# Two graph layers on 32 pairs of graphs: work of the first two and last two rounds reordered on ScalarE, VectorE and GpSimd, degrees of pair 1 found earlier, features asked for at a round's beginning

## The chip, the core and the metric

The kernel runs on one core of one Trainium2 chip. The metric is device time in microseconds of the whole program. Other cores are not used. Engines are named as in the profile: PE is TensorE's matmul (PEld its weight load), DVE is VectorE, ACT is ScalarE, POOL is GpSimd, SP is SyncE, which here only issues DMAs.

## The reference

There are 64 graphs of 256 nodes with 512 features, `x` (64, 256, 512) and `adj` (64, 256, 256), all float32. Two layers, each with a residual:

```
h = relu(layernorm(x));  q, k, v = h Wq^T + bq, h Wk^T + bk, h Wv^T + bv
w = adj * exp(q k^T);    x = x + (w / rowsum(w)) v
h = relu(layernorm(x));  A = adj + I;  d = rowsum(A)^-0.5
x = x + (d A d^T) (h W + b)
```

The output is the last `x`.

## The kernel before

Two graphs make a pair; 32 pairs (`NP`) are worked one after another. All products are float32 on PE. Each product of 2 by 2 blocks is done with seven block products in place of eight (sums before, sums after), so every stage has seven numbered steps; `left_sums` and `right_sums` form the operands, S1 to S4 and t1 to t4.

Stages of a pair, each a function that returns its seven steps:
- `query_stage` (g): gT, the features times a merged query and key weight. Its operands are hT, the turned features, and hS, their sums (`find_feature_sums`). Its results are summed for the next stage by `find_query_sums` (gS).
- `value_stage` (v): v, the values. `find_value_sums` makes two more operands from them, in vS.
- `score_stage` (s): scores, exponentials on ACT (`exponentials`) and the product with `adj` with its row sums on DVE (`mask`). Then `scale_weights` divides by the row sums, `turn_weights` transposes 32 by 32 blocks on DVE (eq), `move_weights` puts these blocks in place with sixteen copies (wT), and `find_weight_sums` makes wS on POOL.
- `output_stage` (o): weights times values, added into x.
- `neighbour_stages` (l and w): the second layer. l is the adjacency (aT, aS) times the second norm's features (h_b, hbS), w that times the weight W, added into x with the factor d.

Around them: `measure` (bn_stats and bn_aggr on DVE, then `inverse_root` and offsets on POOL) and `norm_features` (ACT) make the first layer's h_a in place of the loaded features; `turn_blocks` (DVE, hq) and `move` (sixteen ACT copies) turn it into hT. `measure_again` and `second_norm` do the same for the second layer (st_b, nb_b, h_b), and `find_node_sums` makes hbS. `degrees` sums the rows of `adj` on DVE, finds d on POOL, and by way of a small DRAM tile (dflat, written by SP) spreads d over all partitions (drow, read back by SP); `weigh_degrees` multiplies it with `adj` (ad) and gives ds, the factor of the bias in `add_graph_bias`. `turn_adjacency` transposes `adj` (aq to aT) and asks for the next pair's aq. `find_adjacency_sums` adds the diagonal and makes aS on POOL. `add_value_bias` is a DMA of POOL's queue that adds bv into x.

The order of the work is written by hand. `run` walks a string such as "g1 g5 g6 ..."; each token issues one block product (all of line 514, chained in this order on PE), the copies that read it, and then the calls listed under that token, placed on their engines behind the last instruction that reads a product. Each engine works its queue in order. Round p (`work_around(p)`) runs g, v and s of pair p + 1 with o, l and w of pair p. Ahead of round 0 is a run-in: weights are merged, pair 0 is prepared, and its g, v and s run alone. The last round, p = 30, also holds the O, L and W steps of pair 31, after which nothing is left to overlap. Where the string leaves instructions of one engine free against each other, the scheduler of the language orders them, and it gives buffers: h_a and h_b share three buffers (tag "h"), drow has one, `adj` (a) two, aq one.

Copies matter for the waits: steps 1, 6, 7 and 4 of a stage add into one PSUM bank, and ACT or DVE must have read the bank before the next of them begins.

Of the kernel before, what the change touches and what calls it, by code (L numbers as in the profile page):

```python
# [9 lines left out]
F32 = mybir.dt.float32  # L10
# [6 lines left out]
def kernel(  # L17
# [35 lines left out]
    nc = tc.nc  # L53
    P = 128
    B, N, D = x.shape
    G = 2
    NP = B // G
# [3 lines left out]
    TB = G * NB  # L61
    NT = G * N
# [8 lines left out]
    hp = ctx.enter_context(tc.tile_pool(name="hp", bufs=3))  # L71
# [36 lines left out]
    def load_blocks(p):  # L108

        q_tiles[p] = p1.tile([P, NB, G * N // Q, Q], F32, tag="aq", name=f"aq_{p}")
        blocks = adj[G * p : G * p + G].rearrange(
            "g (j c) (kt i r) -> i c kt (g j) r", c=Q, i=NQ, r=Q
        )
        for i in range(NQ):
            nc.sync.dma_start(q_tiles[p][i * Q : (i + 1) * Q], blocks[i])
# [26 lines left out]

    def load_the_rest():
        load_features(2)
        load_blocks(0)
        load_x(0)
        load_x(1)  # L150
        w1_view = w1.rearrange("(j t p) (i f) -> i j p t f", p=P, t=2, f=HD)
        nc.sync.dma_start(w1_set[:, A11], w1_view[0, 0])
        nc.sync.dma_start(w1_set[:, A12], w1_view[0, 1])
        nc.sync.dma_start(w1_21, w1_view[1, 0])
        nc.sync.dma_start(w1_set[:, A22], w1_view[1, 1])
        nc.sync.dma_start(b1_all, b1.partition_broadcast(P))
# [82 lines left out]
    def transpose_value_weight():  # L239
# [11 lines left out]


    norms, deg, ds, terms, blocks, hTs, parts, second, sides = ({} for _ in range(9))
    gTs, query_parts, weights, row_sums, turned, wTs, weight_parts, value_parts, aTs = (
        {} for _ in range(9)
    )

    def inverse_root(src, plus, name, tag="ir_r"):

# [6 lines left out]
    def scale_offset(xt, name, order, scale=None):  # L266

        mv = sm.tile([P, TB, 2], F32, tag="mv", name=f"mv_{name}")
        for t in order:
            st = sm.tile([P, 6], F32, tag="st", name=f"st_{name}_{t}")  # L270
            nc.vector.bn_stats(st, xt[:, t, :])  # L271
            nc.vector.bn_aggr(mv[:, t, :], st)
        rd = inverse_root(mv[:, :, 1], EPS, name)
        if scale is not None:
            rs = sm.tile([P, TB], F32, tag="rs", name=f"rs_{name}")
            nc.gpsimd.tensor_tensor(rs, rd, scale, mult)
            rd = rs
        nm = sm.tile([P, TB], F32, tag="nm", name=f"nm_{name}")
        nc.gpsimd.tensor_scalar(nm, mv[:, :, 0], -1.0, None, mult)
        nb = sm.tile([P, TB], F32, tag="nb", name=f"nb_{name}")  # L280
        nc.gpsimd.tensor_tensor(nb, nm, rd, mult)  # L281
        return rd, nb
# [12 lines left out]
    def measure(p):  # L295
        norms[p] = scale_offset(feats[p], f"a{p}", range(TB))
# [4 lines left out]
    def measure_again(p):  # L301
        norms[p] = scale_offset(x_tiles[p], f"b{p}", (2, 3, 0, 1), deg[p][0])

    def second_norm(p):
        second[p] = hp.tile([P, TB, D], F32, tag="h", name=f"h_b{p}")
        normed(second[p], x_tiles[p], *norms[p])


    def degrees(p):

        sums = sm.tile([P, TB], F32, tag="deg", name=f"deg_{p}")
        nc.vector.tensor_reduce(sums, a_tiles[p], AX.X, add)
        d = inverse_root(sums, 1.0, f"d{p}", "d")
        flat = dr.tile([NT], F32, tag="drow", name=f"dflat_{p}")
        nc.sync.dma_start(flat.rearrange("(t p) -> p t", p=P), d)
        row = p1.tile([P, NT], F32, tag="drow", name=f"drow_{p}")
        nc.sync.dma_start(row, flat.partition_broadcast(P))
        deg[p] = d, row

    def weigh_degrees(p):  # L320

# [135 lines left out]
    def find_value_sums(p):  # L457

        b11, b21, b22, t1, t2, t3, t4 = value_parts[p]
        eng = nc.gpsimd if p < NP - 1 else nc.vector  # L460
        eng.tensor_tensor(t2, b22, t1, sub)
        last = eng.tensor_tensor(t4, b21, t2, sub)
        if eng is nc.gpsimd:
            read(last)

    def turn_adjacency(p):

# [48 lines left out]
    def read(ins):  # L516
        last_read[ins.ins.engine] = ins.ins
        return ins
# [446 lines left out]
    def work_around(p):  # L965
        work = {
            "g1": [(move_weights, p, 8, 16)],
            "g6": [(find_weight_sums, p), (move, p + 2, 0, 4)],
            "g7": [(move, p + 2, 4, 6)],
            "o5": [(weigh_degrees, p + 1)],  # L970
            "o6": [(move, p + 2, 6, 10), (find_terms, p + 2)],
            "o7": [(move, p + 2, 10, 12), (degrees, p + 2), (add_value_bias, p + 1)],
            "v1": [(move, p + 2, 12, 16)],
            "o3": [(find_adjacency_sums, p), (measure_again, p)],
            "v5": [(find_query_sums, p + 1)],
            "v7": [(second_norm, p), (find_node_sums, p), (load_features, p + 3)],
            "v3": [(find_value_sums, p + 1)],
            "s3": [(load_a, p + 3)],
            "l7": [(measure, p + 3)],
            "l4": [(scale_weights, p + 1)],  # L980
            "l3": [(find_feature_sums, p + 2)],
            "w2": [(turn_weights, p + 1)],
            "w6": [(norm_features, p + 3)],
            "w5": [(turn_adjacency, p + 1)],
            "w7": [(move_weights, p + 1, 0, 8)],
            "w3": [(turn_blocks, p + 3)],
            "w4": [(add_graph_bias, p), (store, p), (load_x, p + 2)],
        }
        if p == 0:

            work["g6"] = [(find_weight_sums, 0)]
            work["g2"] = [(weigh_degrees, 0), (degrees, 1)]
            work["g7"] = []
            work["o5"] = []
            work["o6"] = [(norm_features, 2), (find_terms, 1), (turn_blocks, 2)]
            work["o7"] = [
                (move, 2, 0, 2),
                (add_value_bias, 1),
                (lambda p: weight_sums(w1_set, w1_21, nc.gpsimd), 0),
            ]  # L1000
            work["v1"] = [(move, 2, 2, 10), (weigh_degrees, 1), (degrees, 2)]
            work["v6"] = [(move, 2, 10, 16)]
        if p == 1:
            work["g2"] = [(find_terms, 2)]
        return work
# [2 lines left out]
    bs, g_rows, last = bias_products()  # L1008
    with tc.issue_after(last):
        measure(0)  # L1010
        measure(1)
        degrees(0)
        load_the_rest()
        c_rows, last = weighted_rows(wq_rows, bkT, "U2")
    with tc.issue_after(last):
# [14 lines left out]
        {  # L1030
            "g1": [(lambda p: weight_sums(v_set, v21), 0)],
            "g6": [(norm_features, 1)],
            "g7": [(turn_blocks, 1), (find_terms, 0)],
            "g4": [(move, 1, 0, 6)],
            "g3": [(find_query_sums, 0)],
            "v6": [(move, 1, 6, 7)],
            "s1": [(move, 1, 7, 12)],
            "s3": [
                (move, 1, 12, 16),
                (scale_weights, 0),  # L1040
                (find_feature_sums, 1),
                (turn_weights, 0),
                (load_a, 2),
            ],
            "v7": [(add_value_bias, 0)],
            "v2": [(move_weights, 0, 0, 8)],
            "v4": [(lambda p: nc.scalar.copy(b1_row, b1_all), 0)],
            "v3": [(turn_adjacency, 0), (measure, 2), (find_value_sums, 0)],
        },
    )  # L1050
    for p in range(NP - 2):
# [7 lines left out]
    p = NP - 2  # L1059
    ends = later(neighbour_stages, NP - 1)  # L1060
    run(
# [3 lines left out]
        {**around(p), "O": later(output_stage, NP - 1), "L": ends, "W": ends},  # L1065
        {
# [1 line left out]
            "g6": [(find_weight_sums, p)],  # L1068
            "o5": [(weigh_degrees, p + 1)],
            "o7": [(add_value_bias, p + 1)],  # L1070
            "o3": [(find_adjacency_sums, p), (find_query_sums, p + 1), (measure_again, p)],
            "s3": [(scale_weights, p + 1, nc.vector), (turn_weights, p + 1)],
            "v7": [(second_norm, p), (move_weights, p + 1, 0, 8, nc.gpsimd)],
            "v4": [(find_node_sums, p)],
            "v3": [(move_weights, p + 1, 8, 9), (find_value_sums, p + 1)],
            "l1": [(move_weights, p + 1, 9, 16), (find_weight_sums, p + 1)],
            "l3": [(turn_adjacency, p + 1), (find_adjacency_sums, p + 1)],
            "O3": [(measure_again, p + 1)],
            "w2": [(second_norm, p + 1), (find_node_sums, p + 1)],
            "w7": [(add_graph_bias, p)],  # L1080
            "w4": [(store, p)],
            "L6": [(add_graph_bias, p + 1)],
# [42 lines left out]
```

## Time and profile before

| | |
|---|---|
| median of 3 runs | 1817.01 us (1814.77 to 1819.02) |
| profiled execution | 1822.04 us, its span 1820.3 us |
| PE busy | 1789.2 us (98%), 9978 matmuls |
| DVE, ACT, POOL busy | 1331.5, 1165.2, 1191.4 us |
| mean granted PE clock | 0.996 |
| chain that ended last | PE 91% |

The span runs from the first to the last instruction; 1.7 us of the execution lie outside it. The numbers of a wait row are the total, the count and the longest, in us. A row of the timeline gives start, duration, engine, line, operation, output and inputs, count, and, in brackets, how long the engine was idle before and who ended that. A row of the stretches gives the stretch, its length, busy time and number of instructions of the engine, the granted PE clock, the share of the DMA engines and GB/s. Line numbers are those of the kernel before.

### The profile page before, as it was taken

What the parts mean: (1) busy time and instruction counts of PE and PEld (TensorE: products, weight loads), DVE (VectorE), ACT (ScalarE), POOL (GpSimd) and SP (SyncE); (2) the same over time, 40 slices, a digit from 0 to 9 for tenths busy, and PEclk for the clock granted to TensorE, in tenths of its full rate; (3) what the DMA queues carried; (4) which work ended last, traced back from release to release, by engine and by line L of the source; (5) the groups of instructions that cost most, each with busy time, mean ns of one, the idle gap of its engine ahead of it and who ended that gap; (6) DMA issues with size and microseconds to landing.
All of it is one profiled execution on the core that took longest, in us unless ns stands there. A gap on an engine that the chain in (4) does not pass through costs nothing.

```text
span 1820.3 us, 29061 instructions
## 1 busy us (share of the span) xinstructions
PE 1789.2 (98%) x9978; PEld 1618.9 (89%) x9978; DVE 1331.5 (73%) x3053; ACT 1165.2 (64%) x2326; POOL 1191.4 (65%) x1313
## 2 busy tenths in 40 slices
PE   9989999999999999999999999999999999999997
PEld 8888989999989989989999889999889999899986
DVE  6777777777777678777778787777787777777666
ACT  4765677666677656777666667666766666676532
POOL 2567576676666676766776766776766776766654
PEclk9999999999999999999999999999999999999999
DMA  6623543544543454434445434445435345335321
GB/s 180 150 76 87 113 91 100 114 84 110 111 90 103 103 95 111 100 92 112 97 99 113 94 93 116 86 104 118 85 98 120 76 110 121 83 99 122 64 48 47
DMA packets 245843, 182.58 MB, mean 100 GB/s; under 512 B 155456, under 2 KB 175936, under 8 KB 245696
## 3 DMA queue, kind: packets, MB, share of 16 engines
q1 hardware_dynamic: 227680, 146.11, 28.4%
q0 software_dynamic: 16960, 33.56, 15.0%
q8 instruction: 80, 1.31, 0.3%
q10 hardware_dynamic: 1056, 1.05, 0.2%
q14 instruction: 67, 0.55, 0.1%
HBM read 147.07 MB, written 33.62 MB: 99 GB/s over the span
## 4 chain that ended last, share of the span: by engine, by line
PE 91%; DVE 3%; DMA 2%; ACT 1%; POOL 1%; issue 1%; SPq 0%; DVEq 0%; ACTq 0%; POOLq 0%
PE pm_w L514 21%; PE pm_g L514 20%; PE pm_v L514 20%; PE pm_s L514 10%; PE pm_l L514 10%; PE pm_o L514 10%; DMA h_a<-in_x_dram 1%; DMA dflat<-irr_d 0%; DVE st_a L271 0%; DMA b_qk<-in_L_gnn_Wk_b_dram 0%; DMA drow<-dflat 0%; ACT wT L450 0%; DVE ad L327 0%; ACT h_b L287 0%; DVE st_b L271 0%
## 5 line engine op out<-in xcount | busy, mean ns | idle before, releaser
L514 PE MATMUL pm_w<-w_set,yS 128*128 128x256 f32 x1792 | 401.4, 381 | 8.3 <-DVE yS L879 3.8
L514 PEld LDWEIGHTS pm_w<-w_set,yS 128*128 128x128 f32 x1792 | 336.5, 191 | 53.2 <-DVE yS L879 4.8
L382 ACT COPY hT<-hq 32x512 f32<-32x512 f32 x496 | 305.6, 616 | 8.9 <-DVE hq L363 1.2
L514 PE MATMUL pm_v<-v_set,hT 128*128 128x256 f32 x1024 | 238.2, 381 | 0.8 <-ACT U_v L640 0.8
L514 PE MATMUL pm_g<-hT,m_set 128*128 128x256 f32 x1024 | 236.7, 379 | 0.0
L838 DVE SCALAR_TENSOR_TENSOR x<-pm_w,irr_d,x 128x256 f32<-128x256 f32 x256 | 110.9, 474 | 164.9 <-POOL x L848 113.9
L514 PEld LDWEIGHTS pm_g<-hT,m_set 128*128 128x128 f32 x1024 | 194.6, 190 | 26.9 <-ACT v L247 0.2
L514 PEld LDWEIGHTS pm_v<-v_set,hT 128*128 128x128 f32 x1024 | 193.1, 191 | 26.3 <-ACT U_v L640 1.2
L450 ACT COPY wT<-eq 32x256 f32<-32x256 f32 x504 | 202.3, 401 | 5.9
L514 PE MATMUL pm_v<-v_set,hS 128*128 128x256 f32 x768 | 177.9, 382 | 3.7 <-ACT A_v L649 3.7
L514 PE MATMUL pm_g<-hS,m_set 128*128 128x256 f32 x768 | 176.2, 379 | 0.0
L514 PEld LDWEIGHTS pm_v<-v_set,hS 128*128 128x128 f32 x768 | 144.4, 191 | 22.8 <-ACT A_v L649 4.5
L514 PEld LDWEIGHTS pm_g<-hS,m_set 128*128 128x128 f32 x768 | 146.0, 190 | 19.8
L763 POOL TENSOR_TENSOR x<-x,A_o 128x512 f32<-128x512 f32 x62 | 81.8, 1319 | 111.2 <-ACT A_o L761 110.2
L871 POOL TENSOR_TENSOR yS<-yS,U_l 128x512 f32<-128x512 f32 x32 | 40.7, 1272 | 120.9 <-DVE yS L870 117.1
L689 ACT ACTIVATE e<-e,ks 128x128 f32<-128x128 f32 x192 | 66.5, 395 | 83.0 <-DVE e L727 43.5
L287 ACT ACTIVATE h_b<-x,nb_b,rs_b 128x512 f32<-128x512 f32 x128 | 93.7, 802 | 24.7 <-POOL nb_b L281 24.7
L514 PE MATMUL pm_l<-aT,h_b 128*128 128x128 f32 x768 | 101.3, 275 | 1.7 <-POOL wS L388 1.7
L388 POOL TENSOR_TENSOR wS<-wT 128x256 f32<-128x256 f32 x32 | 23.4, 731 | 121.3 <-ACT wT L450 118.4
L514 PE MATMUL pm_s<-hT,gT 128*128 128x128 f32 x768 | 101.3, 275 | 1.4 <-DVE e L710 1.4
L514 PEld LDWEIGHTS pm_s<-hT,gT 128*128 128x128 f32 x768 | 97.9, 192 | 5.3 <-DVE e L710 2.2
L757 DVE TENSOR_TENSOR x<-pm_o,x 128x512 f32<-128x512 f32 x128 | 87.5, 686 | 18.3 <-PE pm_o L514 17.7
(180 smaller groups left out, 3938.5 us busy)
## 6 DMA issues: line engine op xcount, KB each, us to landing
h_a<-in_x_dram SPq DMA_DIRECT2D x64, 512.0 KB, 7.5
x<-in_x_dram SPq DMA_DIRECT2D x64, 512.0 KB, 4.4
x<-in_L_gnn_Wv_b_dram POOLq DMA_DIRECT2D x32, 1024.0 KB, 11.1
out_dram<-x SPq DMA_DIRECT2D x62, 512.0 KB, 3.5
a<-in_adj_dram SPq DMA_DIRECT2D x64, 256.0 KB, 3.1
aq<-in_adj_dram SPq DMA_DIRECT2D x128, 128.0 KB, 3.6
drow<-dflat SPq DMA_DIRECT2D x32, 256.0 KB, 6.3
wq_w<-in_L_gnn_Wq_w_dram ACTq DMA_DIRECT2D x2, 512.0 KB, 10.3
```

Source lines behind the costliest of these rows:

```text
L287: nc.scalar.activation(h[:, t, :], xt[:, t, :], AF.Relu, bias=nb[:, t : t + 1], scale=rd[:, t : t + 1],)
L382: nc.scalar.copy(dst[j * Q : (j + 1) * Q, i], src[i * Q : (i + 1) * Q, j])
L388: eng.tensor_tensor(s1, a21, a22, add)
L450: copy(dst[j * Q : (j + 1) * Q, i], src[i * Q : (i + 1) * Q, j])
L514: last_product[0] = nc.tensor.matmul(*args, **kwargs).ins
L689: nc.scalar.activation(block(qb, kb)[:, g], scores[:, g], AF.Exp, bias=terms[p][:, t : t + 1])
L757: read(nc.vector.tensor_tensor(block(n, i), bank, block(n, i), add))
L763: read(eng.tensor_tensor(block(n, i), block(n, i), more, add))
L838: nc.vector.scalar_tensor_tensor(to, bank[:, r, :], factor(n, r), to, mult, add)
L871: read(nc.gpsimd.tensor_tensor(t2, b22, t["part"], sub))
```

## The change

- Degrees: `degrees` is cut in two. `degrees(p)` finds d and writes dflat; `spread_degrees(p)` reads it back as drow. In the regular rounds the second half moves from o7 to s3. `degrees(0)` goes ahead of `measure(1)`, tied to the end of the first measuring; `spread_degrees(0)` goes behind feature load 2. `degrees(1)` goes from round 0 to g2 of the run-in, `spread_degrees(1)` and `weigh_degrees(0)` to its v3; `weigh_degrees(1)` and `degrees(2)` go from v1 to o7 of round 0.
- Features: `load_features(p + 3)` goes from v7 to g6. Ahead of it `claim(p)` now takes h_b's tile, which `second_norm` took itself before.
- Run-in: `scale_weights(0)` goes from ACT to DVE; the last four `move` copies of pair 1 and its `find_feature_sums` go from s3 to v7, so behind the copy A_v.
- Round 0: the `move` copies of pair 2 are spread 2, 5, 4, 5 over o7, v1, v6 and v7, where they were 2, 8 and 6 over o7, v1 and v6.
- Last round: v7 comes ahead of v2; the O steps begin between l7 and l3, with a new order among them. `find_value_sums(31)` goes from DVE to POOL. `measure_again(30)` goes from o3 to s6, `second_norm(31)` and `find_node_sums(31)` from w2 to w6, and `find_adjacency_sums(31)` from l3 to w6; the `move_weights` copies of ACT are split 4 and 4 over v3 and l1, where they were 1 and 7.

Of the instructions of PE only the last round's have another order. In the program as built, SP's queue in the run-in and round 0 reads: a(1), dflat(0), features 2, drow(0), aq(0), x(0), x(1), the second layer's weights, dflat(1), features 3, half of aq(1), a(2), the rest of aq(1), drow(1), dflat(2), drow(2), a(3), features 4. Before, it read: a(1), features 2, dflat(0), aq(0) with drow(0) after its first part, x(0), x(1), the weights, most of aq(1), a(2), the rest, dflat(1), drow(1), dflat(2), drow(2), features 3, a(3). In later rounds dflat, drow, features, a, aq keep their places, but the features are one pair further on.

```diff
     def load_the_rest():
         load_features(2)
+        spread_degrees(0)
         load_blocks(0)
...
+    def claim(p):
+
+        second[p] = hp.tile([P, TB, D], F32, tag="h", name=f"h_b{p}")
+
     def second_norm(p):
-        second[p] = hp.tile([P, TB, D], F32, tag="h", name=f"h_b{p}")
         normed(second[p], x_tiles[p], *norms[p])
...
         d = inverse_root(sums, 1.0, f"d{p}", "d")
-        flat = dr.tile([NT], F32, tag="drow", name=f"dflat_{p}")
-        nc.sync.dma_start(flat.rearrange("(t p) -> p t", p=P), d)
+        flats[p] = dr.tile([NT], F32, tag="drow", name=f"dflat_{p}")
+        nc.sync.dma_start(flats[p].rearrange("(t p) -> p t", p=P), d)
+        deg[p] = d, None
+
+    def spread_degrees(p):
+
         row = p1.tile([P, NT], F32, tag="drow", name=f"drow_{p}")
-        nc.sync.dma_start(row, flat.partition_broadcast(P))
-        deg[p] = d, row
+        nc.sync.dma_start(row, flats[p].partition_broadcast(P))
+        deg[p] = deg[p][0], row
...
         b11, b21, b22, t1, t2, t3, t4 = value_parts[p]
-        eng = nc.gpsimd if p < NP - 1 else nc.vector
-        eng.tensor_tensor(t2, b22, t1, sub)
-        last = eng.tensor_tensor(t4, b21, t2, sub)
-        if eng is nc.gpsimd:
-            read(last)
+        nc.gpsimd.tensor_tensor(t2, b22, t1, sub)
+        read(nc.gpsimd.tensor_tensor(t4, b21, t2, sub))
...
-            "g6": [(find_weight_sums, p), (move, p + 2, 0, 4)],
+            "g6": [(find_weight_sums, p), (move, p + 2, 0, 4), (claim, p), (load_features, p + 3)],
...
-            "v7": [(second_norm, p), (find_node_sums, p), (load_features, p + 3)],
+            "v7": [(second_norm, p), (find_node_sums, p)],
             "v3": [(find_value_sums, p + 1)],
-            "s3": [(load_a, p + 3)],
+            "s3": [(spread_degrees, p + 2), (load_a, p + 3)],
...
         if p == 0:
 
-            work["g6"] = [(find_weight_sums, 0)]
-            work["g2"] = [(weigh_degrees, 0), (degrees, 1)]
+            work["g6"] = [(find_weight_sums, 0), (claim, 0), (load_features, 3)]
...
             work["o7"] = [
                 (move, 2, 0, 2),
+                (weigh_degrees, 1),
+                (degrees, 2),
                 (add_value_bias, 1),
                 (lambda p: weight_sums(w1_set, w1_21, nc.gpsimd), 0),
             ]
-            work["v1"] = [(move, 2, 2, 10), (weigh_degrees, 1), (degrees, 2)]
-            work["v6"] = [(move, 2, 10, 16)]
+            work["v1"] = [(move, 2, 2, 7)]
+            work["v6"] = [(move, 2, 7, 11)]
+            work["v7"] = [(move, 2, 11, 16)] + work["v7"]
...
         measure(0)
+        with tc.issue_after(measured[-1]):
+            degrees(0)
         measure(1)
-        degrees(0)
         load_the_rest()
...
+            "g2": [(degrees, 1)],
...
-            "s3": [
-                (move, 1, 12, 16),
-                (scale_weights, 0),
-                (find_feature_sums, 1),
-                (turn_weights, 0),
-                (load_a, 2),
+            "s3": [(scale_weights, 0, nc.vector), (turn_weights, 0), (load_a, 2)],
+            "v7": [(move, 1, 12, 16), (find_feature_sums, 1), (add_value_bias, 0)],
+            "v2": [(move_weights, 0, 0, 8)],
+            "v3": [
+                (turn_adjacency, 0),
+                (weigh_degrees, 0),
+                (spread_degrees, 1),
+                (measure, 2),
+                (find_value_sums, 0),
+                (lambda p: nc.scalar.copy(b1_row, b1_all), 0),
             ],
-            "v7": [(add_value_bias, 0)],
-            "v2": [(move_weights, 0, 0, 8)],
-            "v4": [(lambda p: nc.scalar.copy(b1_row, b1_all), 0)],
-            "v3": [(turn_adjacency, 0), (measure, 2), (find_value_sums, 0)],
...
-        "g1 g5 g6 g2 g7 o1 o5 g4 o6 g3 o2 o7 v1 o4 o3 v5 v6 s1 s6 s5 s7 s2 s4 s3 v2 v7 v4 v3 "
-        "l1 l2 l6 l5 l7 l4 l3 O1 O5 O6 O7 O4 O2 O3 w1 w2 w6 w5 w7 w3 w4 "
+        "g1 g5 g6 g2 g7 o1 o5 g4 o6 g3 o2 o7 v1 o4 o3 v5 v6 s1 s6 s5 s7 s2 s4 s3 v7 v2 v4 v3 "
+        "l1 l2 l6 l5 l7 O1 l4 O5 l3 O6 O2 O7 O3 O4 w1 w2 w6 w5 w7 w3 w4 "
         "L1 L2 L6 L5 L7 W1 L4 L3 W2 W6 W5 W7 W3 W4",
...
-            "o3": [(find_adjacency_sums, p), (find_query_sums, p + 1), (measure_again, p)],
+            "o3": [(find_adjacency_sums, p), (find_query_sums, p + 1)],
+            "s6": [(measure_again, p)],
             "s3": [(scale_weights, p + 1, nc.vector), (turn_weights, p + 1)],
-            "v7": [(second_norm, p), (move_weights, p + 1, 0, 8, nc.gpsimd)],
+            "v7": [(claim, p), (second_norm, p), (move_weights, p + 1, 0, 8, nc.gpsimd)],
             "v4": [(find_node_sums, p)],
-            "v3": [(move_weights, p + 1, 8, 9), (find_value_sums, p + 1)],
-            "l1": [(move_weights, p + 1, 9, 16), (find_weight_sums, p + 1)],
-            "l3": [(turn_adjacency, p + 1), (find_adjacency_sums, p + 1)],
-            "O3": [(measure_again, p + 1)],
-            "w2": [(second_norm, p + 1), (find_node_sums, p + 1)],
+            "v3": [(move_weights, p + 1, 8, 12), (find_value_sums, p + 1)],
+            "l1": [(move_weights, p + 1, 12, 16), (find_weight_sums, p + 1)],
+            "l3": [(turn_adjacency, p + 1)],
+            "O4": [(measure_again, p + 1)],
+            "w6": [
+                (claim, p + 1),
+                (second_norm, p + 1),
+                (find_adjacency_sums, p + 1),
+                (find_node_sums, p + 1),
+            ],
```

More of the change, by code (lines that the diff above doesn't have):

```diff
@@ L253 @@
     norms, deg, ds, terms, blocks, hTs, parts, second, sides = ({} for _ in range(9))
-    gTs, query_parts, weights, row_sums, turned, wTs, weight_parts, value_parts, aTs = (
-        {} for _ in range(9)
+    flats, gTs, query_parts, weights, row_sums, turned, wTs, weight_parts, value_parts, aTs = (
+        {} for _ in range(10)
     )
+    measured = []
     def inverse_root(src, plus, name, tag="ir_r"):
@@ L271, in scale_offset @@
             nc.vector.bn_stats(st, xt[:, t, :])
-            nc.vector.bn_aggr(mv[:, t, :], st)
+            last = nc.vector.bn_aggr(mv[:, t, :], st)
+        measured.append(last.ins)
         rd = inverse_root(mv[:, :, 1], EPS, name)
```

## The prediction

> **What bounds the kernel now.** I read the busy shares first: PE is busy 1789.2 of 1820.3 us, so at most 31.1 us can be won, less what must stay. Then the chain of waits, filtered to PE (total, times, longest):
>
> ```profile
> PE pm_s L514 <- DVE s L336: 4.7, 1, 4.7
> PE pm_w L514 <- DVE yS L879: 3.8, 2, 2.9
> PE pm_v L514 <- ACT A_v L649: 3.7, 2, 2.9
> ...
> PE pm_w L514 <- ACT U_w L847: 3.0, 1, 3.0
> PE pm_l L514 <- POOL wS L388: 1.7, 1, 1.7
> ```
>
> All are single events. By the timeline PE idles 3.5 us at the start, 4.0 at the end, and else at 23.3 (0.8), 54.3 (2.9), 87.7 (0.8), 91.4 (4.7), 171.5 (2.9), 656.7 and 670.6 (0.3, 0.9) and from 1748.7 to 1793.8 in eight pieces (10.3). The rounds between repeat every 54.86 us (pm_g at 239.78 and 294.64) without a gap. So only the edges and two places in the middle can pay.
>
> A gap costs more than its length. By stretches, PE's busy time and granted clock:
>
> ```profile
> 54.30:57.24 2.94, 0.01 (x1) 1.00 1.13 240
> 57.24:62.65 5.41, 5.41 (x17) 0.68 0.58 107
> ...
> 171.46:174.34 2.88, 0.01 (x1) 1.00 0.10 33
> 174.34:176.00 1.66, 1.66 (x4) 0.56 0.00 0
> ```
>
> Sixteen pm_v took 5.41 us where sixteen take 3.45 elsewhere in the chain: 1.96 lost to the clock. Likewise 1.86 after 91.4, 1.96 after 171.5, 2.0 after the pair at 1765 to 1769; nothing after the 3.05 at 1787.4. The Trainium skill (TensorE: Matmul & The Clock Gate, What's actually happening) says the clock halves after an idle window of about 3.4 us, free-running. By it alone only the 4.7 gap would cost extra, about 1.7 us; the rows show four such losses, 7.8 us. I take the rows: a gap near 3 us costs 1.9 more, three times in four.
>
> **First pair (ScalarE).** v4 at 54.3 waits for A_v, queued on ACT behind four hT moves (2.50) and four row scalings (1.70). The scalings go to VectorE (1.14 in the last round's row), the moves behind A_v. The exponentials end at 52.47 and v7 at 52.4, so A_v ends at 53.1, before 54.3: 2.9 + 1.96 = 4.9 won. Cover: the moves now end at 55.6, g1 starts at 57.65; eq is done at 55.8, the sixteen wT moves at 63.35, before o1 at 66.3. Four scalings delay VectorE's v sums, which it catches up by 63.5; a late hT move would cost PE what it exceeds 2.1 us by.
>
> **Degrees of pair 1 (VectorE, GpSimd, SP).** The gS sums of round 0 stood behind weigh_degrees(1):
>
> ```profile
> 75.90 8.43 DMA dflat<-irr_d
> 84.35 7.20 DMA drow<-dflat
> ...
> 91.56 0.96 DVE ad L327 x2
> ```
>
> The reduction (1.2) moves to g2 of the run-in, where VectorE idles 1.40 at 35.2: free. On SP, dflat(0) now stands ahead of feature load 2, which goes from 13.8 to about 21.6, needed at 66.4: free. Then drow(0), aq, x, weights come about 7 us sooner; dflat(1) is asked at about 43 and landed by 53. Then SP holds feature load 3 (its buffer, pair 0's, is free at 43.3), aq(1), a(2), and only then drow(1). a(2) waits for the last ad of pair 0, now at about 67 behind the transposes of aq and between bn_stats; so drow(1) is asked at 69.5 and lands at 76.7. VectorE reaches its first ad at 79.5. The row is no longer late; what is queued in VectorE is: four hc, four hq, deg(2) 78.1, four bn_stats and ad, then gS to 85.5. s6, 5.0 sooner than in the trace plus the 0.8 at 87.7 (U_v, now behind five hT moves of 0.62, not eight), is due at 85.4. It waits up to 1 us.
>
> **What is late next: h_b of round 0.** In a regular round PE arrives at s7 as VectorE frees its bank, at the end of a fixed run behind nb_b:
>
> ```profile
> 154.17 2.93 ACT L287 ACTIVATE h_b<-x,nb_b,rs_b 128x512 f32<-128x512 f32 x4 [1.58 <-POOL nb_b L281]
> ...
> 157.00 0.35 ACT L706 COPY e<-pm_s 128x256 f32<-128x256 f32 x1
> ...
> 157.38 0.42 DVE L710 TENSOR_TENSOR e<-pm_s,e 128x256 f32<-128x256 f32 x1 [1.22 <-ACT e L706]
> ...
> 157.88 1.14 PE L514 MATMUL pm_s<-hT,gT 128*128 128x128 f32 x8
> ```
>
> That is nb_b + 3.9. In round 0, GpSimd runs the four w1 sums, irr_d and the adjacency sums before nb_b: 81.92 to 93.1 in the trace, 11.2 us. In the new order irs_d(2) stands ahead of them and waits for deg(2) at 78.1, so they run 78.4 to 89.5, and nb_b (2.8, as at 650.46) is ready at 92. s7 starts at about 96, where it started at 103.19: 7.2 won over both gaps, less 1.9 for a clock that again halves after a gap of some 4 us. Net 5.3 by round 0's end (uncontended GpSimd and no clock loss: 8.5; one more us of everything: 3). Even with nb_b early, ACT's five hT moves behind A_v at v7 hold e to 91.5 and s7 to 92.
>
> **Features at g6, all rounds.** The 2.9 + 1.96 at 171.5 and 0.9 + 0.3 at 670.6 are st_a waiting for h_a, asked behind a drow that waits for dflat (13.7 and 11.8 us to land). Asked a round ahead, it has about 50 us of slack: 6.1 won in the profiled execution. The request waits for the last reader of h_b (l4) and holds a and aq behind it on SP: a is asked some 4 us later, lands in 3 to 6 us, and is read over 25 us on. The row's drow, now issued at s3, waits for the same landing as before and is first read in the next round. Free while that slack stands. Orders on ACT, VectorE and GpSimd in rounds 2 to 29 are unaltered.
>
> **The last two rounds.** The gS sums come ahead of bn_stats: the 1.1 at s7 goes, but the four bn_stats (2.65) now hold e717/e718 to 51.85 (of 17xx), s3 is due at 51.25: 0.65 back. v7 ahead of v2 covers A_v: 0.7 won. With find_value_sums off VectorE, U_l comes 1.2 sooner (two sums of 0.6); I find 0.35 at l6 and 0.6 at l7 in place of 1.75. O1 and O5 between l7, l4 and l3 cover 0.77 and, with shorter gaps, the 2.0 of slow clock; O2 and O3 between the others cover 0.77 and 0.68 (an output product takes 0.86, its copy 0.76). w1 then starts at 1773.0, not 1780.5: 7.5 won. U_w ahead of h_b removes the 3.05 at w7.
>
> What takes it back: find_adjacency_sums(31) now stands on GpSimd between two x sums, and the second half of add_graph_bias on VectorE waits for the later one, with U_l and so L7 behind it. nb_b 80.4, x sum 81.7, two diagonals 1.4, four aS, x sum 1.27, then on VectorE two bias adds 1.4, four x sums 1.76, yS and U_l 1.2. Here a rule speaks against the change. GpSimd's rows:
>
> ```profile
> 1742.58 0.73 POOL L400 TENSOR_TENSOR aS<-aT 128x256 f32<-128x256 f32 x1
> 1743.39 1.17 POOL L401 TENSOR_TENSOR aS<-aT,aS 128x256 f32<-128x256 f32 x1
> ```
>
> 0.73 alone, 1.17 beside a VectorE sum. The Trainium skill (SBUF — State Buffer, SBUF: two separate sides) calls the port pair of the two an exclusive lock: aS and hbS would run in turn, 4 x 0.7 + 4 x 0.6 = 5.2 us. By the rows aS takes 4.3, with no overlap 2.75. So U_l ends at 1791.9 to 1794.3; I take the rows, 1793.2. L7 is due at 1789.5: a gap of 3.7, with its clock loss 5.6. L7 starts at about 1793.2 instead of 1801.2: 8.0 less 1.5 (1.9 at three in four) leaves 6.5; ends 3.5 and 10.
>
> **Sum.** 5.3 + 6.1 + 6.5 = 17.9 from the profiled execution's 1822.04: 1804.1. The runs' median, 1817.01, lies 5.0 lower. The row's dflat took 7.5 to 13.7 us from issue to landing, so the gaps at 171.5 and 670.6 may be smaller in those runs; I count half of them, 3: 1817.0 - 5.3 - 6.5 - 3.0 = 1802.2, rounded to 1802. The runs before spread over 4.3 us; 0.2% (3.6 us) is about what a measurement can tell from no change.
>
> **Rivals.**
> (a) The covers hold: nb_b of round 0 and U_l of round 31 come in time, gaps under 1 us without clock loss. For it: both chains are sums of ten terms, and GpSimd waits little for VectorE if their operations interleave. Against: the eleven us of GpSimd work is measured. Gains: 4.9 + 0.8 + 6.5 - 1 in round 0, 12.3 at the end, 3 to 5: 1791.
> (b) The same waits, but larger, and the feature gaps not in the median runs at all: 3 + 3.5 + 0: 1810.5. For it: 5.0 between profile and median. Against: only three of the dflat landings that the trace shows took over 11.7.
> (c) Slower: the features' request blocks SP. If it waits past the next round's o7, a is late for degrees and PE for gS in each of 30 rounds. At 0.5 us a round it eats the 11.8 won and passes +0.2%; at 0.7 the time is 1826. Against: more than 25 us of slack.
> (d) Nothing moves: each wait has a successor of its size: 1817.
>
> **Chances.** Forecast 0.52, (a) 0.22, (b) 0.18, (c) 0.04, (d) 0.04. Faster 0.92, same 0.04, slower 0.04. The range takes in the bounds (8.5 and 10 give 1795; 3 and 3.5 without features 1810.5) and most of (a): 1791 to 1810.
>
> **What would show it.** No PE gap at 54; at 88 to 96 one gap of 3 to 4.5 before pm_s behind L710, with nb_b near 92; no st_a wait for h_a; O and l products without gaps; one gap of 3 to 4 before L7's pm_l behind U_l, slow clock after both. Wrong if either of these two gaps is missing, if a middle round grows past 54.86, or if SP holds drow(1) past 80.

## The result, and the profile after

| | before | after |
|---|---|---|
| median | 1815.8 us (5 runs, 1814.8 to 1819.0) | 1810.2 us (5 runs, 1808.8 to 1810.6) |
| ratio, 95% interval | | 0.9964, 0.9949 to 0.9978 |
| profiled execution, its span | 1822.04, 1820.3 us | 1809.05, 1806.8 us |
| PE idle in the span, mean granted clock | 31.1 us, 0.996 | 20.3 us, 0.997 |

The change gains 5.6 us by the medians (4.0 to 9.3 by the interval), where 14.8 was forecast from a median of 1817.0. The forecast of 1802 is 8.2 us too low, and 1810.2 lies just outside its range. The profiles tell another story than the runs: between the two profiled executions lie 13.0 us.

The chain of waits of the changed kernel, filtered to PE (total, times, longest):

```profile
PE pm_l L522 <- DVE U_l L869: 6.3, 2, 3.6
PE pm_s L522 <- DVE gS L400: 3.5, 1, 3.5
...
PE pm_s L522 <- DVE e L718: 1.4, 2, 1.1
PE pm_w L522 <- ACT U_w L855: 0.6, 1, 0.6
```

The waits for A_v at 54.3 and for yS behind st_a are gone, and that for U_w has shrunk from 3.0 to 0.6. VectorE is now behind nearly everything: gS ahead of s6 in round 0, and U_l twice, ahead of l7 and L7 in the last round. The stretches of these three gaps and what follows them (stretch, length, then the busy time of PE, PEld, DVE, ACT and POOL; the granted clock is the third number from the end):

```profile
85.09:88.64 3.55, 0.00 (x1) 0.03 (x1) 3.55 (x9) 2.89 (x5) 3.39 (x4) 1.00 0.06 2
88.64:94.00 5.36, 5.36 (x25) 4.64 (x26) 3.50 (x5) 1.25 (x2) 3.75 (x7) 0.68 0.33 49
1752.43:1755.16 2.73, 0.00 (x2) 0.03 (x1) 2.48 (x3) 0.00 (x0) 2.65 (x4) 1.00 0.00 0
1755.16:1760.00 4.84, 4.84 (x23) 4.43 (x24) 1.27 (x2) 1.43 (x3) 2.47 (x3) 0.65 0.00 0
1782.58:1786.18 3.60, 0.01 (x2) 0.03 (x1) 3.50 (x8) 0.00 (x0) 0.00 (x0) 0.98 0.26 97
1786.18:1792.00 5.82, 5.82 (x30) 5.42 (x31) 3.18 (x5) 1.86 (x4) 1.63 (x2) 0.72 0.32 120
```

Behind each, the mean clock over about 5 us is 0.65 to 0.72: some 1.7 us more apiece. PE's w1 of round 0 starts at 109.08, in the profile of before at 114.74: 5.7 won. The last round begins at 1711.0, before at 1722.7: 11.7 won, so 6.0 more from the feature waits. From there to the end it is 95.8 us against 97.6: only 1.8 won.

VectorE beside GpSimd in round 0, as the timeline shows each (start, duration, engine, line, operation):

```profile
79.44 0.41 DVE L338 SCALAR_TENSOR_TENSOR ad<-a,drow 128x256 f32<-128x256 f32 x1
...
80.44 1.41 DVE L338 SCALAR_TENSOR_TENSOR ad<-a,drow 128x256 f32<-128x256 f32 x1
...
81.87 0.65 DVE L274 BATCH_NORM_STATS2 st_b<-x 128x6 f32<-128x512 f32 x1
82.45 0.81 DVE L338 SCALAR_TENSOR_TENSOR ad<-a,drow 128x256 f32<-128x256 f32 x1
...
83.87 1.49 DVE L338 SCALAR_TENSOR_TENSOR ad<-a,drow 128x256 f32<-128x256 f32 x1
...
85.38 1.10 DVE L399 TENSOR_TENSOR gS<-gT 128x512 f32<-128x512 f32 x1
```

```profile
80.31 1.26 POOL L178 TENSOR_TENSOR w_set<-w_set,wq_w 128x512 f32<-128x512 f32 x1
81.53 1.45 POOL L177 TENSOR_TENSOR w_set<-w_set 128x512 f32<-128x512 f32 x1
...
83.81 1.26 POOL L179 TENSOR_TENSOR w_set<-w_set 128x512 f32<-128x512 f32 x1
```

The same `ad` takes 0.41 us at 79.44, where GpSimd runs only irr_d, an operation of 4 elements a partition, and up to 1.49 beside a w1 sum of GpSimd. It is not slowed at random: the sums end at 81.57, 82.98 and 85.07, and the three `ad` end at 81.85, 83.26 and 85.36, each 0.28 or 0.29 later. So they behave as if their work began when the sum is over. `bn_stats`, in the middle of one of the sums, keeps its 0.65. The three slow `ad` cost 1.00 + 0.40 + 1.08 = 2.48 us; s6's gap of 3.55 less these is 1.07.

And in the last round, ahead of l7 at 1755.16, first VectorE and then GpSimd:

```profile
1750.18 1.76 DVE L401 TENSOR_TENSOR h_b<-h_b 128x512 f32<-128x512 f32 x1
1751.87 1.75 DVE L402 TENSOR_TENSOR hbS<-h_b,hbS 128x512 f32<-128x512 f32 x1
```

```profile
1749.80 1.60 POOL L471 TENSOR_TENSOR vS<-v,vS 128x512 f32<-128x512 f32 x1
1751.48 1.59 POOL L472 TENSOR_TENSOR vS<-v,vS 128x512 f32<-128x512 f32 x1
```

`find_value_sums(31)` left VectorE's queue and holds it up from GpSimd: each of the two hbS sums beside it (the first writes over a part of h_b) ends 0.54 or 0.55 us after the GpSimd sum, and takes 1.76 and 1.75 in place of the 0.68 of an undisturbed one. The excess is 2.15 us; the gap of 2.73 less 2.15 is 0.58.

### The profile page after: what moved, and what is told of

Read it like the earlier page. It is cut to its first block, busy times and chain, and to the rows that moved or that the text cites. A ratio compares the mean times of both kernels' runs of the same rounds, so it can differ in the third digit from the quotient of the medians.

```text
span 1806.8 us, 29092 instructions
## 1 busy us (share of the span) xinstructions
PE 1786.5 (99%) x9978; PEld 1617.6 (90%) x9978; DVE 1338.1 (74%) x3055; ACT 1163.6 (64%) x2322; POOL 1194.9 (66%) x1315
## 4 chain that ended last, share of the span: by engine, by line
PE 93%; DVE 4%; issue 1%; ACT 1%; POOL 1%; DVEq 0%; ACTq 0%; POOLq 0%
PE pm_w L522 21%; PE pm_g L522 20%; PE pm_v L522 20%; PE pm_l L522 11%; PE pm_s L522 11%; PE pm_o L522 10%; PE pm_mT L197 1%; DVE ad L338 1%; DVE st_b L274 1%; DVE hc L364 0%; DVE x L765 0%; ACT e L697 0%; PE pm_run_in L189 0%; DVE gT L579 0%; ACT h_b L291 0%
## 5 line engine op out<-in xcount | busy, mean ns | idle before, releaser
L522 PEld LDWEIGHTS pm_l<-aT,h_b 128*128 128x128 f32 x768 | 94.9, 195 | 7.0 <-issue 4.0
```

What stands on the lines that cost most here:

```text
L522: last_product[0] = nc.tensor.matmul(*args, **kwargs).ins
```

## Experiments

Four theories had to be told apart: the feature waits are an event of one execution or of all; round 0's gaps come from GpSimd's w1 sums or from the degrees; l7's gap comes from GpSimd beside hbS or from U_l's own chain; L7's gap comes from the adjacency sums' place. Each group of four runs stood beside its own runs of the kernel before, and each of the three groups ran on another chip, so differences are taken within a group where that is possible.

### The parts alone

**Features alone**, in the kernel before:

```diff
-            "g6": [(find_weight_sums, p), (move, p + 2, 0, 4)],
+            "g6": [(find_weight_sums, p), (move, p + 2, 0, 4), (claim, p), (load_features, p + 3)],
...
-            "v7": [(second_norm, p), (find_node_sums, p), (load_features, p + 3)],
+            "v7": [(second_norm, p), (find_node_sums, p)],
```

> The kernel before with one edit: h_b is claimed and features p+3 are asked for at g6 instead of v7; the first two and the last two rounds are as before. Theory A (the two feature gaps of the profile of before, worth 6.1 us, are an event of that one execution: its drow had landed late by chance): the median of the timed runs is that of the kernel before, 0 within 1.5 us, while the profile of this kernel shows no st_a wait and ends about 6 us sooner than the profile of before, if that is profiled again as it was. Theory B (they stand in all runs): 4 to 6 us faster. The forecast's half: 3.

Measured: 1814.9 us (1813.5 to 1817.7) beside 1821.8 for the kernel before (27 runs, 1817.1 to 1827.2); ratio 0.9963 (0.9951 to 0.9975), so 4.6 to 8.9 us. No st_a wait in the profile. Theory A is refuted for this group of runs: asking earlier pays in the timed runs too. But the kernel before itself now needed 6 us more than in the first comparison. That both come from a longer wait is likely but not shown: none of the 27 executions has a profile, and the chip is another cause that no run separates.

**The run-in and round 0 alone**: the changed kernel with the last two rounds of before, features asked for at v7, drow at s3.

```diff
-            "g6": [(find_weight_sums, p), (move, p + 2, 0, 4), (claim, p), (load_features, p + 3)],
+            "g6": [(find_weight_sums, p), (move, p + 2, 0, 4)],
...
-            "v7": [(second_norm, p), (find_node_sums, p)],
+            "v7": [(second_norm, p), (find_node_sums, p), (load_features, p + 3)],
```

> The change in the run-in and round 0 alone, with drow asked at s3 as the change has it; features are asked for at v7 and the last two rounds are as before. By the profiles of before and after, w1 of round 0 starts 5.7 us sooner: 5 to 6 us faster in the timed runs if the gain stays to the end. Rival: part of it is given back in the rounds between, because a and the features of the next pairs are then late: under 3 us. If the feature gaps come from drow's place on SP, the profile shows an st_a wait here too, perhaps in other rounds than 171 and 670 us.

Measured: 1816.7 (1811.4 to 1818.3) beside the same 1821.8: 5.1 us, ratio 0.9963 (0.9949 to 0.9976). The gain of round 0 stays to the end. The st_a wait is here, at 166.1, and it is 3.6 us long, with a stretch of slow clock of 6.8 us that begins in it: moving drow to s3 did not free the features, since both still stand behind the landing of dflat. SP's queue in round 2:

```profile
145.29 0.37 SPq L319 DMA_DIRECT2D dflat<-irr_d  x1
157.99 0.34 SPq L325 DMA_DIRECT2D drow<-dflat  x1
158.42 1.29 SPq L101 DMA_DIRECT2D h_a<-in_x_dram  x2
```

drow waits 12.3 us for dflat, and h_a stands behind it. Two of the six runs took 1811.4 and 1812.2 at a granted clock of 0.999, the four others 1816.0 to 1818.3 at 0.995 to 0.996. A wait with its slow clock in some runs and a short one in the others would do this; only one of the four has a trace.

**The last two rounds alone**, in the kernel before, `find_value_sums(31)` on GpSimd included:

```diff
-        "g1 g5 g6 g2 g7 o1 o5 g4 o6 g3 o2 o7 v1 o4 o3 v5 v6 s1 s6 s5 s7 s2 s4 s3 v2 v7 v4 v3 "
-        "l1 l2 l6 l5 l7 l4 l3 O1 O5 O6 O7 O4 O2 O3 w1 w2 w6 w5 w7 w3 w4 "
+        "g1 g5 g6 g2 g7 o1 o5 g4 o6 g3 o2 o7 v1 o4 o3 v5 v6 s1 s6 s5 s7 s2 s4 s3 v7 v2 v4 v3 "
+        "l1 l2 l6 l5 l7 O1 l4 O5 l3 O6 O2 O7 O3 O4 w1 w2 w6 w5 w7 w3 w4 "
...
-        eng = nc.gpsimd if p < NP - 1 else nc.vector
-        eng.tensor_tensor(t2, b22, t1, sub)
+        nc.gpsimd.tensor_tensor(t2, b22, t1, sub)
```

> The change in the last two rounds alone, find_value_sums(31) on GpSimd included; run-in, round 0 and the features as before. By the profiles of before and after, from the last round's start to the end: 1 to 2.5 us faster, with gaps of 2.5 to 3 at l7 and 3.6 at L7. Rival (the forecast's 6.5, the l7 gap being an event of one execution): 5 to 7 us faster, with l7's gap under 1.

Measured: 1820.2 (21 runs), ratio 0.9988 (0.9980 to 0.9996): 0.7 to 3.6 us. The gaps at l7 and L7 are 2.72 and 3.60, as in the changed kernel. So this part is worth about 2 us (1.6 by the medians), not 6.5, and its gaps are no event of one execution.

### Round 0: the w1 sums on GpSimd

First the sums were only moved, to v2 of the run-in, where GpSimd has nothing to do for 12 us:

```diff
-                (lambda p: weight_sums(w1_set, w1_21, nc.gpsimd), 0),
...
-            "v2": [(move_weights, 0, 0, 8)],
+            "v2": [(move_weights, 0, 0, 8), (lambda p: weight_sums(w1_set, w1_21, nc.gpsimd), 0)],
```

> The changed kernel with one edit: the four w1 weight sums on GpSimd stand at v2 of the run-in, where GpSimd idles, and no longer at o7 of round 0 ahead of nb_b. Theory (these sums set nb_b and slow VectorE's ad to 1.4 us, and so make both the gap of 3.55 at s6 and that of 1.1 at s7): nb_b 4 to 5 us sooner, both gaps together under 1.5, about 4 to 5 us faster than the changed kernel, so 9 to 11 faster than the kernel before. Rival 1 (deg(2) and irs_d(2) set them, the sums only follow): nb_b is under 1.5 us sooner and the time within 1.5 of the changed kernel's. Rival 2 (the five hT moves on ScalarE come next): s7 at about 92, gaps of 2 to 3 together, 2 to 3 us faster.

Measured: 1808.6 beside 1821.8, ratio 0.9924 (0.9912 to 0.9936). Its span of 1804.9 is 1.9 under that of the changed kernel, not 4 to 5. The theory's first half holds: nb_b came at 89.2 and not 92.5, s6's gap is 0.95 and no slow clock follows; s7's 1.11 stayed. But the sums took their lock along. In the run-in they fell on the masks of VectorE (GpSimd first):

```profile
52.79 1.33 POOL L179 TENSOR_TENSOR w_set<-w_set 128x512 f32<-128x512 f32 x1
```

```profile
52.93 1.48 DVE L707 SCALAR_TENSOR_TENSOR e<-e,a 128x256 f32<-128x256 f32 x1
...
54.34 0.41 DVE L707 SCALAR_TENSOR_TENSOR e<-e,a 128x256 f32<-128x256 f32 x1
```

The last mask takes 0.41, once GpSimd is quiet; the other three take 0.94, 1.14 and 1.48 beside the sums. v's sums came 2.6 us later, and PE waited 2.29 at v of the run-in. Here an idle engine was not a free place, since its neighbour was busy.

Then they were taken off GpSimd. VectorE idles 1.86 and 1.34 us between the v sums of round 0, and a sum takes 0.68 there:

```diff
-                (lambda p: weight_sums(w1_set, w1_21, nc.gpsimd), 0),
...
+            work["v7"] = work.get("v7", []) + [(lambda p: first_sums(w1_set, w1_21), 0)]
+            work["s5"] = work.get("s5", []) + [(lambda p: last_sums(w1_set, w1_21), 0)]
```

`first_sums` and `last_sums` are two and two of the four sums of `weight_sums`, on VectorE.

> The changed kernel with one edit: the four w1 weight sums on VectorE in two pairs (v7 and s5 of round 0), GpSimd's queue freed of them. Theory (on GpSimd they slowed VectorE's ad and with it gS and s6): gap at s6 0.9 instead of 3.55, no slow clock behind it, s7's 1.1 unchanged since e717/e718 there waits for VectorE's own order; 4 to 5 us faster than the changed kernel, as the run with three edits gained more than its two others together. Rival (half of the 9.7 of the three comes from elsewhere, as from slow clock at the end): under 3.

Measured: 1804.6 (1803.8 to 1805.0) beside 1818.1, ratio 0.9929 (0.9917 to 0.9941); the changed kernel needed 1810.2 and 1808.9 in its two groups of runs. Span 1802.5 against 1806.8 and 1807.4: 4.3 to 4.9. s6's gap is 0.95, the clock behind it 1.00, s7's 1.11 as before. Three of the four `ad` take 0.41; only the last, beside an adjacency sum, takes 0.95. From s6's gap to w1 of round 0 PE needs 15.84 us, in the two profiles of the changed kernel 20.31: this 4.5 is the edit's. The rest is chance that nearly cancels: this execution comes to s6 0.7 to 1.0 later, a lag that it has from 34 us on, and its last round is 0.8 to 1.1 shorter, since no slow clock follows the same gap of 2.73 at l7. The first theory holds, with its size, and rival 1 of the run above falls. Of rival 2 the gaps came (0.95 and 1.11, together 2) and the 2 to 3 us did not; what s7 waits for is not ScalarE, which has its e at 92.24, but VectorE, which takes v's last sum at 92.56 and e at 93.17.

### The last round: value sums and adjacency sums

These three runs and one of the changed kernel itself stood beside 11 runs of the kernel before with a median of 1816.9 (1813.0 to 1822.8).

> The changed kernel as it is, beside new runs of the kernel before on the chip of the three runs below. In the first comparison it gained 5.6 us (1815.8 to 1810.2), while its profile ended 13.0 us ahead of the profile of before. Theory C (the feature waits are in most runs of the kernel before but were missing from some of those five; without them the run-in, round 0 and the last rounds leave 6 to 7.5): where the kernel before needs about 1821 to 1822 us, the gain is 12 to 14. Rival D (the feature request costs something in the changed kernel that the runs of the single parts do not show): the gain stays at 5 to 7 beside a kernel before of 1821.

Measured: the changed kernel at 1808.9 (1807.7 to 1810.4), ratio 0.9953 (0.9936 to 0.9970): 8.1 us, 5.5 to 11.6 by the interval. The kernel before did not need the 1821 that either theory spoke of, so neither is decided by this run. What it shows is that the changed kernel stays within 1807.7 to 1810.6 in both groups, while the kernel before moves between 1813 and 1823 in the same two.

**Value sums of pair 31 back on VectorE:**

```diff
-        nc.gpsimd.tensor_tensor(t2, b22, t1, sub)
-        read(nc.gpsimd.tensor_tensor(t4, b21, t2, sub))
+        eng = nc.gpsimd if p < NP - 1 else nc.vector
+        eng.tensor_tensor(t2, b22, t1, sub)
+        last = eng.tensor_tensor(t4, b21, t2, sub)
```

> The changed kernel with the two value sums of pair 31 back on VectorE. Theory (at l7 the two hbS sums on VectorE ran 1.76 us each beside GpSimd's vS sums, where they take 0.6 to 0.7 alone; that is the gap of 2.7 at l7 and the slow clock after it): the gap at l7 falls to 0.6 to 1.8 and its clock loss of 1.9 goes or stays with it; 1.5 to 3.5 us faster than the changed kernel from the last round's start to its end, if L7 behind it does not wait longer. Rival (U_l is late for another reason: the PSUM bank, ScalarE): the gap stays at 2.5 to 3. Second rival (the end is set by U_l for L7 on its own chain): what is won at l7 is lost at L7, whose gap grows by as much; the time stays.

Measured: 1807.0, so 1.9 less than the changed kernel beside it. VectorE's queue ahead of l7:

```profile
1750.28 0.68 DVE L401 TENSOR_TENSOR h_b<-h_b 128x512 f32<-128x512 f32 x1
1750.88 0.68 DVE L402 TENSOR_TENSOR hbS<-h_b,hbS 128x512 f32<-128x512 f32 x1
1751.48 0.68 DVE L472 TENSOR_TENSOR vS<-v,vS 128x512 f32<-128x512 f32 x1
```

The hbS sums are back at 0.68. The gap at l7 is 1.58, though VectorE has two sums more to do there, and the clock behind it stays at 1.00; w1 starts 2.7 us sooner on the same beginning. L7's gap stays at 3.60, but the slow clock behind it now lasts 6.83 us in place of 3.41, which takes part of it back. The theory holds, both rivals fall.

**Adjacency sums of pair 31 back at l3:**

```diff
-            "l3": [(turn_adjacency, p + 1)],
+            "l3": [(turn_adjacency, p + 1), (find_adjacency_sums, p + 1)],
...
-                (find_adjacency_sums, p + 1),
                 (find_node_sums, p + 1),
```

> The changed kernel with the adjacency sums of pair 31 on GpSimd back at l3, ahead of nb_b and both x sums. Theory (they stand between the two x sums that U_l of L7 waits for): the gap of 3.6 at L7 falls under 1 and the slow clock behind it goes; 3.5 to 5.5 us faster than the changed kernel. Rival (moved forward, they delay nb_b, h_b and hbS by as much as they took): the gap turns up ahead of L1 or stays at 2 to 3.6; under 1.5 us faster.

Measured: 1806.7, so 2.2 less than the changed kernel. That is short of the theory's 3.5 and above the rival's 1.5: L7's gap falls from 3.60 to 1.69 and nothing slow follows it, but the gap at w7 grows from 0.62 to 1.53. GpSimd does the sums ahead of nb_b, which comes 0.9 later on the same beginning; U_w stands behind h_b on ScalarE, and h_b behind nb_b.

**All three edits together** (w1 on VectorE, value sums on VectorE, adjacency sums at l3):

> The changed kernel with three edits: value sums of pair 31 on VectorE, adjacency sums of pair 31 at l3, and the four w1 weight sums on VectorE in two pairs (at v7 and s5 of round 0, where VectorE idles 1.9 and 1.3 us) instead of on GpSimd at o7. If the three causes are separate and add up: gaps at s6 and s7 of round 0 together about 2 instead of 4.7 without slow clock (4 us), l7 and L7 as in the two runs above (1.5 to 3.5 and 3.5 to 5.5): 9 to 12 us faster than the changed kernel. Rival (each stall removed leaves one of its size behind it): under 6.

Measured: 1799.2 (1799.1 to 1800.0), ratio to the kernel before 0.9901 (0.9884 to 0.9917), and 9.7 us less than the changed kernel beside it: within the 9 to 12, so the causes are separate. The single edits gave 1.9, 2.2 and 4.2 to 5.6, together 8 to 10. It beats both kernels. Its waits of PE:

```profile
...
PE pm_l L533 <- DVE U_l L880: 3.3, 2, 1.7
PE pm_w L533 <- ACT U_w L866: 1.6, 1, 1.6
```

Between the start and the end no gap is over 1.7 us; PE idles 15.8 us in place of 20.3 to 20.5, and the mean granted clock is 1.000 in place of 0.997. The gaps give 4.7 us of the 9.7; the clock, 0.003 of 1807, the other 5. No slow clock is left between start and end, where the changed kernel has three stretches of it.

### The kernel before, three times more

> The kernel before, unchanged, profiled again. If the feature waits come and go with the landing of dflat (12 to 14 us in the executions that waited), the profile's end follows them: about 1815 to 1816 without a wait ahead of st_a, 5 more with the wait of round 2 and its slow clock, 1 to 2 more for a second one. If the waits always stand as in the first profile (gaps of 2.9 at 171 and 1.2 near 670), every look ends at 1821 to 1823.

> As the run ahead of it: the kernel before again, for another landing of dflat. A wait of under 1 us ahead of st_a at 170, or none, should go with an end of 1814 to 1817; a wait of 2.5 or more with 1820 to 1823.

> As the two runs ahead of it. Over the three, PE's gap behind L7's and round 2's st_a should be the only place where the middle rounds differ; the rounds of 54.86 us stay.

Measured: 1816.4, 1817.3 and 1817.5 us, spans 1814.6, 1815.5 and 1814.9, where the first profile had 1820.3. The wait behind st_a in round 2 stands in all three, but PE's gap is 1.30, 1.35 and 1.54 in place of 2.88, no slow clock follows it, and the second one near 670 is missing. SP's queue in the first of the three:

```profile
150.89 0.37 SPq L315 DMA_DIRECT2D dflat<-irr_d  x1
163.26 0.34 SPq L317 DMA_DIRECT2D drow<-dflat  x1
```

drow follows dflat by 12.4 us, in the first profile by 13.8 (150.64 to 164.42). A landing 1.4 us later made the wait 1.6 us longer, and there the clock halved behind it: 1.3 became 4.8, and 6.0 with the second wait. The landing of the features adds to it: in the run of the run-in and round 0 alone, drow followed dflat by 12.7, but the second half of h_a took 8.0 us, in these four profiles 5.7 to 6.4, and PE waited 3.64. So neither theory is right as it stood: in every profile of a kernel that asks at v7 the wait is there, but its price runs from 1.3 to 6.8 with these landings and the clock. I had thought the middle rounds the only place to differ; round 0 differs too: its gaps of 0.82 and 4.0 in two of the three are 0.60, 1.93 and 1.06 in the third.

## Why the prediction was wrong

**First pair and round 0: the sum right, the cause not.** Forecast 5.3, shown by the traces 5.7, by the part alone 5.1. The right total was luck. The gaps and their clock came to 2.9 + 2.0 + 0.8 + 4.7 + 1.9 = 12.3 before and 0.2 + 3.55 + 1.7 + 1.1 + 0.1 = 6.65 after. A_v's wait went as forecast; irs_d(2), drow(1), nb_b and s7 came within 1 us of the forecast times (nb_b at 92.5 for 92, s7 at 96.9 for 96). But the step "It waits up to 1 us" at s6 failed. It became 3.55, of which 2.48 is the excess of three `ad` beside the w1 sums; the gap of some 4 us that I put at s7 behind nb_b was met ahead of s6. I had listed those sums among what delays nb_b, and not asked what they do to VectorE meanwhile. The run with the sums on VectorE shows what that was worth: 4 to 5 us.

**Features: the mechanism right, the term not one number.** No round of the changed kernel waits for h_a, a lands in time, and the middle rounds stay at 54.86 (one takes 55.44, as one does in the kernel before). In the trace 6.0 were won for 6.1. For the median I counted half, 3. In the three later profiles of the kernel before the wait is 1.3 to 1.5; in the first it cost 6.0, in the run of the run-in and round 0 alone 6.8. The request alone gained 6.9 by the medians where the kernel before took 1821.8. That the first comparison's runs of before had the short wait was not seen, as they have no profile of their own; their 1814.8 to 1819.0 fit it. With 1.4, the parts are 5.7 + 1.4 + 1.8 = 8.9 us, inside the interval of both comparisons (4.0 to 9.3 and 5.5 to 11.6); why the first gave 5.6 by its medians and the second 8.1 stays open. Beside the 1821.8 of the first group, where the changed kernel was not run, it would gain some 12 (an estimate: 1821.8 less its 1808.9 to 1810.2).

**The last two rounds: here the forecast fell.** Forecast 6.5, shown 1.8, by the part alone 0.7 to 3.6. (Over more profiles it is 1.6: from the last round's beginning to the end six with the old order take 96.2 to 98.6 us, 97.5 on the mean, five with the new one 95.2 to 96.2, 95.9 on the mean.) The step that failed is "With find_value_sums off VectorE, U_l comes 1.2 sooner (two sums of 0.6); I find 0.35 at l6 and 0.6 at l7 in place of 1.75", and with it "the 2.0 of slow clock" that was to be avoided at l7. The gap was 2.73, and the clock halved behind it: 2.1 and 2.0 us more than forecast, nearly all of the 4.7 that are missing; w1 came 2.75 sooner, not 7.5. Without the excess of the two locked sums the gap would be 0.58, as forecast; with the value sums back on VectorE those sums were at 0.68 again, and neither the gap of 2.73 nor the slow clock came. I had costed the move as a saving on VectorE and at nothing on GpSimd. The rule of one lock for both engines I had quoted: I weighed it for the adjacency sums alone, where the rows (1.17 to 1.23 for a sum of 0.73) gave the better figure, and did not carry it to the two places where VectorE was on PE's path. There it held: hbS sum and vS sum ran one after the other, as the Trainium skill has it for a VectorE operation with two SBUF inputs (SBUF — State Buffer, SBUF: two separate sides). The rows that I took for the price were of GpSimd's side, which loses 0.4 to 0.5; the side that waited for the whole sum is VectorE's. The profile of before had such a row too, in the run-in, with a vS sum itself:

```profile
61.28 1.63 POOL L461 TENSOR_TENSOR vS<-v,vS 128x512 f32<-128x512 f32 x1 [9.69 <-DVE vS L654]
61.70 1.76 DVE L402 TENSOR_TENSOR hT<-hT 128x512 f32<-128x512 f32 x1
```

The VectorE sum, 0.68 beside nothing, ends 0.55 after GpSimd's: the same 1.76 as at l7. And beside the very aS rows that I quoted, VectorE's gS sums took 1.22 and 1.21 (at 1745.09 and 1746.23). It could be read before the forecast, and I had not priced the move by it.

**L7, U_w and the products without gaps: right.** L7's gap is 3.60 for 3.7, slow clock behind it; w7's 3.05 is 0.62; the O products stand without gaps and s3's gap is 0.37.

**Clock.** "A gap near 3 us costs 1.9 more, three times in four" held as a rate (15 of 20, below), with 1.7 by the granted clock for 1.9. It is why small misses cost double: three gaps of the changed kernel carry over 5 us of slow clock. But which gap pays is not a toss for each gap by itself; it follows from where the gap lies, as the last section works out.

**Rivals.** (b), the same waits but larger and no feature gaps in the median runs, at 1810.5, is the number that came, but by other terms: round 0 gave 5.7 for its 3, the last rounds 1.8 for its 3.5, the features more than its 0. (c) did not happen: SP is not blocked. (Its 0.5 us a round, 15 in all, less 11.8 leaves 3.2, just short of the 0.2% that it was to pass.) (a) had the right covers in mind; the kernel with three edits reaches 1799.2 by taking away what uncovered them.

## What to carry to other kernels

Before moving element-wise work from VectorE to GpSimd, read what VectorE does on PE's path in that window: here its operations with two SBUF operands waited for the whole of a running GpSimd sum, and the move cost more (2.15 us) than the work it saved (1.2). Where VectorE itself has idle stretches between PSUM reads, the work is cheaper there, at 0.68 us a sum for 1.27. And when the profiled execution lies above the median, profile the kernel before a few times more: a wait behind a DMA's landing had another price in each execution here, and the clock can turn a gap that grows from 1.5 to 3 us into a loss of 5. Where a gap cannot be closed it can still pay to bring it under 1.9 us: no gap below that was followed by slow clock by itself.

## What the runs showed of the hardware that was not expected

The lock of the two engines was known, its price was not. Of VectorE's operations beside a GpSimd sum, those with two SBUF operands end 0.28 us (`ad`, 0.41 undisturbed) or 0.54 us (hbS sums, 0.68 undisturbed) after the sum does, wherever in its time they were issued; `bn_stats`, with one, is not touched. GpSimd's sum, 1.27 alone, takes up to 1.60 in the meantime.

PE's clock after gaps, counted over the 14 profiled executions by the granted clock in the 7 us behind each gap (the start apart): after gaps of 1.0 to 1.7 us it fell in none of 28; of 1.75 to 2.3 in 5 of 11; of 2.7 to 3.1 in 15 of 20; of 3.5 to 4.7 in 15 of 15. The same gap of 3.05 at w7 cost nothing in three executions of before's last rounds and 1.5 to 3.0 in three others.

What decides is where the gap lies. The Trainium skill names a free-running window of about 3.4 us (TensorE: Matmul & The Clock Gate, What's actually happening), and the traces show it: within each trace all slow stretches begin on one grid of 3.413 us, to 2 ns, and last 3.41 us (28 of them) or 6.83 (6). With that grid laid over a trace, PE's idle time in each window tells what comes. The gap of 2.73 at l7 in the changed kernel, and the same gap in the run with the w1 sums on VectorE (window, length, PE's busy time, granted clock):

```profile
1751.91:1755.32 3.41, 0.68 (x6) 1.00 0.00 0
1755.32:1758.73 3.41, 3.41 (x13) 0.50 0.00 0
```

```profile
1747.03:1750.45 3.42, 1.94 (x16) 1.00 0.00 0
1750.45:1753.86 3.41, 2.17 (x15) 1.00 0.00 0
1753.86:1757.27 3.41, 3.41 (x25) 1.00 0.00 0
```

In the first the gap lies in one window, and the next runs at half clock; in the second it falls into two, 1.48 and 1.24, and costs nothing. Over the 14 traces (start and end apart) a window with 1.92 us or more of idle was followed by half clock in 34 of 34 cases, one with 0.5 to 1.89 in none of 90. A slow window that itself had 0.66 us or more of idle was followed by a second one (6 of 6), one with 0.50 or less never. So a window need not be idle as a whole, as the page has it. One slow window costs 1.7 us (half of 3.41). Two short gaps in one window count together, as the 1.75 at 1765 and part of the 0.77 behind it did in the first profile of before (2.25). The chances above are those of a gap's place on the grid.
